# Layer 1 of a two-layer metaformer: silu(z) ahead of the scans, gating of each group at its end, output projection of five groups during the last passes

## The chip, the cores and the metric

The kernel runs on one core of one Trainium2 chip. The metric is the device time of one execution in microseconds (us). A stated time is the median of several executions. In the profile PE is TensorE (matmul), PEld its weight load, DVE is VectorE, ACT is ScalarE, POOL is GpSimd, and SP issues most of the DMAs. PEclk is the clock granted to TensorE as a share of full speed. A name such as L1216 is a line of the kernel whose profile is read; the two kernels have different line numbers.

## The reference

Two layers, each a two-dimensional state space block with a gate, then an MLP in simulated fp8. The change touches only the gate and the output projection of layer 1:

```python
# x: 1 x 64 x 64 x 96, D_INNER = 192, 16 states, L = 64*64 = 4096
def _L1_conv_ref(x, W_in, conv_w, conv_b, x_proj_w, dt_proj_w, dt_proj_b, A_logs, Ds, W_out):
    xz = x @ W_in.T
    xp, z = (xz[..., :D_INNER], xz[..., D_INNER:])
    xc = jax.nn.silu(conv3x3(xp) + conv_b)            # full 192 x 192 convolution
    # four directions: rows, columns, and both reversed
    # dts, Bs, Cs: projections of xc; delta = softplus(dts + dt_proj_b)
    # h = exp(delta*A)*h + (delta*u)*B ; y = sum over states of h*C, + Ds*u
    yy = y[0] + wh_y + inv_y[0] + invwh_y             # [..] directions summed
    yy = yy * jax.nn.silu(z)
    return yy @ W_out.T
# [..] then x = x + that, and t = t + ffn(layernorm(t))
```

## The kernel before

Layer 1 has four parts: convolution and projections, a stretch in which the first operands of the scans are loaded, 24 scan passes (six groups of 32 channels times four quarters of the states), and the tail. Constants: `P=128, L=4096, CH=512, NCH=8, SC=1024, NS=4, NG=6, NK=4, NQ=4, GC=32, CD=96, DI=192`. In a pass, 16 scans of 128x1024 run on VectorE; ScalarE makes the decays, GpSimd multiplies by B and C, and TensorE adds the four directions and folds the states into an accumulator `accs[g]`.

```python
def layer1(self, w):
    # [..] pools: up (u, xd, dtc), ps (2 PSUM), pc (4 PSUM), kp (sg), sp (z, dt, du, zz, p; 2 buffers each)
    for c in range(0, NCH, 4):
        self.conv_chunks(kp, ps, pc, u, c)
        self.project_chunks(sp, ps, u, c)      # u, dt, du, B, C to DRAM
    for g in range(2):
        nc.sync.dma_start(self.dt_d[1][g * P : g * P + GP[g], :], self.dtc[g])

def scans(self):
    # [..] st: dt0, dt1, du, x0..x2, xw, c, hs, h0, h1 of [P, L], three hc of [P, SC]
    def store(i):                              # y of a group to DRAM at the group's end
        g, k = passes[i]
        if k < NK - 1:
            return
        t = hcs[(NS * i + NS) % 3].rearrange("p (b t) -> p b t", t=CH)
        keep(nc.scalar.copy(t, accs[g]))
        to = self.y_d[GC * g : GC * g + GC, :].rearrange("c (b q t) -> q c b t", q=NQ, t=CH)
        for q in range(NQ):
            nc.sync.dma_start(to[q], t[GC * q : GC * q + GC])
    # [..] plan: which helper is issued after which scan of a pass

def tail(self, w, out):
    # [..] u, y and the layer's input xt are loaded back from DRAM
    def gate(c):
        s = chunk(c)
        for g in range(2):
            n = GP[g]
            nc.vector.scalar_tensor_tensor(
                y[g][:, s], u[g][:, s], self.tail_d4[g][0:n], y[g][:, s], ALU.mult, ALU.add)
            z = self.pa.tile([P, CH], F32, tag="a", name=f"z1{c}{g}")
            self.keep(nc.tensor.matmul(z[0:n], w_in[:, g * P : g * P + n], xt[:, s], start=True, stop=True))
            sg = self.tp.tile([P, CH], F32, tag="sg", name=f"sga{c}{g}")
            nc.scalar.activation(sg[0:n], z[0:n], AF.Sigmoid)
            nc.vector.tensor_tensor(sg[0:n], sg[0:n], z[0:n], ALU.mult)
            nc.gpsimd.tensor_tensor(y[g][:, s], y[g][:, s], sg[0:n], ALU.mult)
    def mixed(c):                              # output projection of one chunk of 512 tokens
        o = self.po.tile([P, 4, CD], F32, tag="o", name=f"o1{c}")
        for j in range(4):
            at = slice(c * CH + j, (c + 1) * CH, 4)        # every fourth token is a weight column
            for g in range(2):
                self.keep(nc.tensor.matmul(o[:, j, :], y[g][:, at], w_out[g], start=g == 0, stop=g == 1))
        nc.vector.tensor_tensor(self.res[:, c], self.res[:, c], o, ALU.add)
        self.mlp_norm(1, c)
    for c in range(NCH):
        gate(c)
    # [..] for each chunk in turn: mixed, mlp_turn (transpose), mlp_up, mlp_down, store
```

`keep` holds an instruction to the program order on its engine; what is not kept, the scheduler may move.

## Time and profile before

The kernel before takes 1683.67 us (1680.88 to 1685.94, three runs). The profiled execution has a span of 1672.6 us. I cut it where one thing becomes the next.

| stretch (us, profiled execution) | from | length |
|---|---|---|
| first store of dt of the last chunks to the issue of the load of x0s | 517.99 | 28.5 |
| issue of x0s to the first scan | 546.46 | 32.6 |
| the 24 passes of scans | 579.11 | 931.0 |
| end of the last scan to the last sum of states | 1510.13 | 19.2 |
| last sum of states to the end | 1529.36 | 143.2 |

The other lines of this profile on which the argument rests stand in the prediction below. A row of a timeline is: start, length, engine and line, operation, output and inputs, shapes, number of instructions; in brackets the idle time of the engine just ahead and what ended it. One more line of this kernel is from the view of a single source line and gives the shortest, median and longest duration in ns of the weight loads with which TensorE adds the directions inside the scans:

```profile
L1190 PEld LDWEIGHTS hs<-hss,ident x384: 186/190/338, 601.0 to 1522.1; 128*128 128x128 f32 x192
```

A load of 128 neighbouring columns takes 0.19 us here, wherever TensorE has its full clock (301 of the 384 loads), and 0.29 to 0.34 us where the granted clock is 0.50 (70 of them).

### The profile page before, as it was taken

Reading aid. Unit: us, or ns where it says so; the run is one execution under the profiler, and the core shown is the slowest. Engines: PE = TensorE matmul, PEld = TensorE weight load, DVE = VectorE, ACT = ScalarE, POOL = GpSimd, SP = SyncE. Lnnn points to the kernel's source line nnn. Section 1 sums busy time; section 2 is a strip of 40 time slices with the busy share of each in tenths; the row PEclk is TensorE's granted clock in tenths of the full one; section 3 lists DMA queues with packets and bytes.
Section 4 is the critical chain, followed back from the end, with each engine's and each line's share of the span. In section 5 each row is a group of like instructions: output and inputs, shape, how many; then the busy total and the mean of one; then the engine's idle time right before and its main releaser. Section 6 shows DMA issues by size and latency. Waiting matters only on the chain.

```text
span 1672.6 us, 11637 instructions
## 1 busy us (share of the span) xinstructions
PE 1199.6 (72%) x3518; PEld 487.2 (29%) x3518; DVE 1203.2 (72%) x921; ACT 874.5 (52%) x988; POOL 780.4 (47%) x435
## 2 busy tenths in 40 slices
PE   5969788799992047776667777677777666776986
PEld 2512344443430012222222222222222222222353
DVE  6595355400505199999999999999999999991634
ACT  5233243301405366667676777766676667752233
POOL 1001222100202447777777666777777687642522
PEclk9968766599995568888888787888888788888555
DMA  2121200001204802454355345433633563213400
GB/s 68 50 71 49 50 10 10 19 13 32 88 26 148 348 26 101 173 201 127 127 195 170 126 151 187 127 107 144 218 122 108 180 224 117 59 55 82 119 10 29
DMA packets 52011, 178.37 MB, mean 107 GB/s; under 512 B 18288, under 2 KB 23140, under 8 KB 44772
## 3 DMA queue, kind: packets, MB, share of 16 engines
q1 hardware_dynamic: 50356, 177.35, 32.3%
q8 instruction: 29, 0.48, 0.1%
q10 hardware_dynamic: 1584, 0.20, 0.1%
q14 instruction: 42, 0.34, 0.1%
HBM read 154.92 MB, written 22.56 MB: 106 GB/s over the span
## 4 chain that ended last, share of the span: by engine, by line
DVE 43%; PE 26%; ACT 6%; DMA 5%; issue 4%; POOL 3%; SPq 2%; DVEq 1%; POOLq 0%; ACTq 0%
DVE h0s L1173 13%; DVE h1s L1173 12%; DVE xws L1173 6%; PE cv L974 4%; DVE x0s L1173 4%; DVE x2s L1173 3%; DVE x1s L1173 3%; PE o L1336 3%; ACT da L1161 2%; PE cv L979 2%; PE z L1323 2%; PE cw L987 2%; DMA cs<-bc 2%; PE in L285 1%; PE o L455 1%
## 5 line engine op out<-in xcount | busy, mean ns | idle before, releaser
L1190 PE MATMUL hs<-hss,ident 128*128 128x512 f32 x384 | 233.5, 694 | 132.7 <-POOL hss L1179 87.2
L1161 ACT ACTIVATE da<-dt0s,a 128x1024 f32<-128x1024 f32 x168 | 187.7, 1117 | 137.5 <-DVE xws L1173 52.3
L1161 ACT ACTIVATE da<-dt1s,a 128x1024 f32<-128x1024 f32 x168 | 187.9, 1119 | 102.7 <-DVE xws L1173 69.6
L1179 POOL TENSOR_TENSOR hss<-h1s,xws 128x1024 f32<-128x1024 f32 x96 | 224.4, 2374 | 26.7 <-PE hs L1190 14.2
L1173 DVE TENSOR_TENSOR_SCAN xws<-da,xws 128x1024 f32<-128x1024 f32 x96 | 224.2, 2335 | 8.3
L1191 PE MATMUL hs<-h0s,ident 128*128 128x512 f32 x384 | 216.5, 648 | 5.1 <-DVE h0s L1173 5.1
L1173 DVE TENSOR_TENSOR_SCAN h1s<-da,h1s,xws 128x1024 f32<-128x1024 f32 x72 | 169.2, 2350 | 9.7 <-ACT da L1161 0.5
L1190 PEld LDWEIGHTS hs<-hss,ident 128*128 128x128 f32 x384 | 75.5, 215 | 274.4 <-issue 101.6
L1191 PEld LDWEIGHTS hs<-h0s,ident 128*128 128x128 f32 x384 | 81.0, 211 | 114.7 <-issue 103.4
L1203 POOL TENSOR_TENSOR hc0s<-hc0s,cs 128x1024 f32<-128x1024 f32 x32 | 75.3, 2355 | 79.9 <-ACT hc0s L1198 65.6
L1203 POOL TENSOR_TENSOR hc1s<-hc1s,cs 128x1024 f32<-128x1024 f32 x32 | 75.4, 2355 | 77.2 <-ACT hc1s L1198 65.8
L1203 POOL TENSOR_TENSOR hc2s<-hc2s,cs 128x1024 f32<-128x1024 f32 x32 | 75.3, 2354 | 76.3 <-ACT hc2s L1198 67.0
L1049 POOL TENSOR_TENSOR du<-u,dt 128x1024 f32<-128x1024 f32 x6 | 17.4, 2896 | 198.9 <-ACT z L691 109.8
L1214 PE MATMUL acc<-hc0s,fold 128*32 128x512 f32 x128 | 40.6, 719 | 75.2 <-POOL hc0s L1203 75.2
L1214 PE MATMUL acc<-hc1s,fold 128*32 128x512 f32 x128 | 40.6, 719 | 73.9 <-POOL hc1s L1203 73.9
L1144 POOL TENSOR_TENSOR x0s<-x0s,dus 128x1024 f32<-128x1024 f32 x32 | 75.0, 2355 | 34.4 <-DMA dus<-du 24.0
L1173 DVE TENSOR_TENSOR_SCAN h1s<-da,xws 128x1024 f32<-128x1024 f32 x24 | 54.5, 2271 | 48.6 <-DMA cs<-bc 45.6
L1214 PE MATMUL acc<-hc2s,fold 128*32 128x512 f32 x128 | 39.7, 704 | 68.6 <-POOL hc2s L1203 68.6
L1144 POOL TENSOR_TENSOR x2s<-x2s,dus 128x1024 f32<-128x1024 f32 x32 | 75.1, 2359 | 14.9 <-DMA cs<-bc 9.1
L1144 POOL TENSOR_TENSOR x1s<-x1s,dus 128x1024 f32<-128x1024 f32 x32 | 75.0, 2356 | 12.3 <-DMA cs<-bc 8.2
L1150 ACT COPY xws<-x0s 128x1024 f32<-128x1024 f32 x32 | 61.5, 1951 | 31.8 <-POOL x0s L1144 31.8
L1173 DVE TENSOR_TENSOR_SCAN x1s<-da,x1s 128x1024 f32<-128x1024 f32 x32 | 74.7, 2335 | 2.8
(245 smaller groups left out, 2433.7 us busy)
## 6 DMA issues: line engine op xcount, KB each, us to landing
cs<-bc SPq DMA_DIRECT2D x384, 128.0 KB
x0s<-bc SPq DMA_DIRECT2D x32, 512.0 KB
x1s<-bc SPq DMA_DIRECT2D x32, 512.0 KB
x2s<-bc SPq DMA_DIRECT2D x32, 512.0 KB
dus<-du SPq DMA_DIRECT2D x24, 512.0 KB
dt1s<-dt SPq DMA_DIRECT2D x40, 256.0 KB
dt0s<-dt SPq DMA_DIRECT2D x40, 256.0 KB
bce<-re SPq DMA_DIRECT2D x2, 1232.0 KB
```

The lines of the kernel that those rows point to most:

```text
L974: nc.tensor.matmul(t, cw[0][:, tap, 0:P], image(0, slice(0, P), n, tap), start=tap == 0, stop=False)
L979: nc.tensor.matmul(t, cw[1][r, tap, 0:P], image(1, r, n, tap), start=False, stop=tap == 8)
L1144: keep(nc.gpsimd.tensor_tensor(x, x, du[:, part[j]], ALU.mult))
L1150: keep(nc.scalar.copy(grid(xw)[:, w, :], cols(xs[i % 3])[:, w, :]))
L1161: nc.scalar.activation(das[i, s], dt[o][:, part[j]], AF.Exp, scale=self.a6[:, g, k : k + 1])
L1173: keep(nc.vector.tensor_tensor_scan(to, da, x, start, ALU.mult, ALU.add))
L1179: nc.gpsimd.tensor_tensor(cols(hs)[:, w, :], grid(first[1])[:, w, :], grid(xw)[:, w, :], ALU.add)
L1190: keep(nc.tensor.matmul(t, self.ident, hs[:, s], start=True, stop=False))
L1191: keep(nc.tensor.matmul(t, self.ident, first[0][:, s], start=False, stop=False))
L1203: keep(nc.gpsimd.tensor_tensor(t, t, c[:, part[j]], ALU.mult))
L1214: nc.tensor.matmul(accs[g][GC * q : GC * q + GC, m // NQ, :], self.fold4, hcs[(NS * i + a) % 3][:, h * CH : (h + 1) * CH], start=k == 0, s ...
L1336: nc.tensor.matmul(o[:, j, :], y[g][:, at], w_out[g], start=g == 0, stop=g == 1)
```

## The change

Two idle places were to be used. Between the projections and the first scan TensorE has nothing to do, so z, its sigmoid and their product move there and go to DRAM (`gate1`). During the scans TensorE and GpSimd have slack, so each group is gated at its own end, and the output projection of groups 0 to 4 runs in the last three passes. The tail keeps the projection of the last group's 32 channels and the MLP. To make room, C gets two tiles of a quarter of the length instead of one full tile.

```diff
@@ layer1
+            xt = zp.tile([CD, L], F32, tag="xt", name="xt1z")
+            nc.scalar.dma_start(xt, self.xn_d)
             for c in range(0, NCH, 4):
                 self.conv_chunks(kp, ps, pc, u, c)
                 self.project_chunks(sp, ps, u, c)
             # [..] stores of dtc
+            self.gate1(kp, sp, ps, xt)
+        # [..] in project_chunks, keep(...) around ScalarE's column copies of dt
+
+    def gate1(self, kp, sp, ps, xt):
+        # [..] silu: sigmoid on ScalarE (kept in order), product with z on VectorE
+        for i in range(6):
+            g = i // 4
+            sz = sp.tile([P, n], F32, tag="z", name=f"sz{i}")
+            for m in range(2):
+                t = ps.tile([P, CH], F32, tag="ps", name=f"z1{i}{m}")
+                # [..] one matmul, or two of 64 rows
+                silu(sz[:, m * CH : (m + 1) * CH], t, f"{i}{m}")
+            # [..] nc.scalar.dma_start(self.sz_d[..], sz[..])
@@ scans
-            xw, c, hs = (st.tile([P, L], ...) for t in ("xw", "c", "hs"))
+            xw, hs = (st.tile([P, L], ...) for t in ("xw", "hs"))
+            cs = [st.tile([P, SC], F32, tag=f"c{m}", name=f"c{m}s") for m in range(2)]
+            def load_gate(i, late): ...          # u and silu(z) of the group into gu, gz
+            def skip(i): ...                     # ScalarE: gu = gu * 4D
+            def fetch_y(i):
+                    keep(nc.scalar.copy(t, accs[g]))
+                    keep(nc.gpsimd.tensor_tensor(gu, gu, t, ALU.add))
             def store(i):
-                keep(nc.scalar.copy(t, accs[g]))
+                    keep(nc.gpsimd.tensor_tensor(gu, gu, gz, ALU.mult))
+                    # [..] gu to y_d
+            def early_out(m):
+                t = ph.tile([P, CH], F32, tag="hs", name=f"eo{m}")
+                for j in range(4):
+                    keep(nc.tensor.matmul(o[:, j], gu[:, b, j:CH:4], w0, start=True, stop=False))
+                    keep(nc.tensor.matmul(o[:, j], gz[0:GC, b, j:CH:4], w1, start=False, stop=True))
+            def early_fetch(m): ...              # ScalarE: PSUM to et
+            def early_add(m): ...                # GpSimd: res += et
+            def gate_last(i, a): ...             # VectorE: last group, a quarter at a time
+            at(gate_last, 18, 20, 23, 29)
-            at(load_c, 2, 5, 7, 13)
+            at(load_c, 7, 13, 17, 20)
+                    for f, at_slots in ((early_out, (8, 10, 11)), (early_add, (12, 13, 14)), (early_fetch, (9, 11, 13))):
+                        # [..] in passes 21, 22 and 23: three, three and two chunks
@@ tail
-            # [..] reloads of u, xt and y; gate(c) for all chunks
             def mixed(c):
                 for j in range(4):
-                    for g in range(2):
-                        nc.tensor.matmul(o[:, j, :], y[g][:, at], w_out[g], ...)
+                    nc.tensor.matmul(o[:, j, :], y[r, b, j:CH:4], w2[r], start=True, stop=True)
```

## The prediction

> **What bounds the kernel now.** I read the table of busy time by stretch first, with the cuts set where the chain of waits changes engine: convolution and projections of layer 1, the bubble before the first scan, the 24 scan passes, the last sums, the gate, and output projection with MLP.
>
> ```profile
> core 0: us, PE busy (x) PEld busy (x) DVE busy (x) ACT busy (x) POOL busy (x), PEclk, DMA share, GB/s
> 514.00:579.00 65.00, 0.00 (x0) 0.00 (x0) 19.17 (x14) 22.16 (x17) 27.28 (x11) 0.50 0.75 281
> 579.00:1510.00 931.00, 642.96 (x1489) 240.30 (x1490) 892.00 (x384) 639.57 (x619) 643.77 (x277) 0.83 0.41 139
> 1510.00:1530.00 20.00, 16.87 (x48) 6.06 (x46) 0.13 (x1) 4.02 (x7) 8.32 (x4) 1.00 0.00 0
> 1530.00:1574.00 44.00, 31.43 (x33) 6.49 (x33) 23.65 (x31) 10.66 (x17) 19.40 (x15) 0.51 0.77 191
> 1574.00:1673.00 99.00, 69.99 (x280) 48.60 (x280) 39.98 (x82) 32.19 (x66) 23.67 (x35) 0.50 0.04 16
> ```
>
> The scans (579 to 1510) are DVE alone: 384 scans in 931 us, 2.42 us from one to the next, 38.8 us for a pass of 16. The waits of DVE in that stretch confirm it:
>
> ```profile
> DVE h1s L1173 <- DMA cs<-bc: 45.6, 1, 45.6
> DVE h1s L1173 <- ACT da L1161: 3.5, 7, 0.6
> ```
>
> Only 3.5 us are lost inside; the 45.6 us are the wait for the first scan. PE, ACT and POOL are 69% busy there, so each has some 11 us free in a pass. What is left to win lies at the two ends. The timeline of PE shows the back end:
>
> ```profile
> 1528.31 1.05 PE L1214 MATMUL acc<-hc2s,fold 128*32 128x512 f32 x4 [2.50 <-POOL hc2s L1203]
> 1542.52 31.40 PE L1323 MATMUL z<-xta,tw_in 96*128 96x512 f32 x32 [13.16 <-DMA xta<-xn]
> 1573.85 11.43 PE L1336 MATMUL o<-two,ys 128*128 128x96 f32 x32
> 1591.32 0.66 PE L171 MATMUL tf<-identb,xb 128*96 128x128 bf16 x4 [6.04 <-POOL xb L1403]
> ...
> 1646.78 5.70 PE L1336 MATMUL o<-two,ys 128*128 128x96 f32 x16
> 1654.96 0.66 PE L171 MATMUL tf<-identb,xb 128*96 128x128 bf16 x4 [2.48 <-POOL xb L1403]
> ```
>
> From the last sum of states (1529.4) to the end (1672.6) are 143.2 us: 13.2 of reloading, 31.4 of z products, then the output projection, 16 instructions and 5.5 us for each of 8 chunks, in turn with the MLP. The front end, from the timelines of SP, POOL, ACT and DVE:
>
> ```profile
> 538.71 1.13 SPq L949 DMA_DIRECT2D dt<-dtc  x1
> 546.46 2.39 SPq L1117 DMA_DIRECT2D x0s<-bc  x4
> ...
> 559.87 9.23 POOL L1144 TENSOR_TENSOR x0s<-x0s,dus 128x1024 f32<-128x1024 f32 x4 [23.97 <-DMA dus<-du]
> ...
> 569.13 7.46 ACT L1150 COPY xws<-x0s 128x1024 f32<-128x1024 f32 x4 [31.77 <-POOL x0s L1144]
> ...
> 579.11 2.29 DVE L1173 TENSOR_TENSOR_SCAN h1s<-da,xws 128x1024 f32<-128x1024 f32 x1 [45.64 <-DMA cs<-bc]
> ```
>
> This is a serial chain: the load of x0s waits until the store of dtc frees its memory, and 32.6 us later (579.11 - 546.46) the first scan starts. PE does nothing here, ACT and DVE nothing from 538. So the bubble looks free for the gate, but only if x0s doesn't wait for it.
>
> **What the Trainium skill says.** "TensorE: Matmul & The Clock Gate", Part 1, has the array at half rate by default and after an idle window of some 3.4 us, and at full rate after as long a busy one. The trace agrees on the first half: 1.00 up to 1530, then 13.2 us idle, then 0.51. On the second it doesn't: 31 us of z products never raised it. I therefore price both new z products and the tail at the half clock. The same page, Part 2, step by step, says that a weight load's time follows the columns, not the rows; the trace agrees (the 6x128 and the 128x128 loads both took 0.18 to 0.19 us at full clock), so 32 rows in place of 128 and 64 make the projection cheaper by fewer instructions, not by cheaper ones. "ScalarE: Activation LUTs", What ACT_TABLE_LOAD costs, gives 1283 ns for a table; the trace has 1.28 us. The front has sigmoid's table already, so one load leaves the tail and none is added. "DMA: Bandwidth & Descriptors", Anatomy of one DMA, puts most of a fixed 2 us into the receipt of the write; I use it for the sz stores, as no row gives landing times.
>
> **The change part by part.**
>
> Tail, removed or moved. The reload and z products vanish: 1573.85 - 1529.4 = 44.4 us. The projection keeps only the last group's 32 channels: 8 instructions a chunk, not 16, so 8 x 0.344 (5.5 / 16) = 2.75 us. First two chunks: before, 17.5 us from 1573.85 to the first turn at 1591.32; after, 5.5 of products, and most of the norm, some 9 in all (the gate of the last quarter, two DVE operations of 0.7, runs beside the products). Turns one to seven: before 1654.96 - 1591.32 = 63.6 us, less six projections of 2.75, 47.1. But here the norm hid beneath a projection; in the built program the normalisation of every second chunk still stands behind the next chunk's residual add on DVE, so the 2.48 us wait before the turn stays and its neighbour gets one too: I add 4, 51. The end, 1654.96 to 1672.6, stays 17.6. Sum 9 + 51 + 17.6 = 78, against 143: **-65**.
>
> Front, added. The order of the built program and its semaphores settle this. PE's z products may run early, but ACT's sigmoids are kept behind the last dtc copy (ends 537.4). Twelve tiles, two PSUM buffers: at half clock a tile costs PE 1.7 us (two instructions of 0.85; before the tail made one in 1.95), sigmoid 0.6 and multiply 0.7 beside it, plus an ACT DMA issue a pair: about 3.5 us a pair, six pairs, 21, to 558.5. Two sz buffers mean that a pair also waits for the store two earlier, 512 KB among the 5 MB that already saturate the DMA until 546; that gives much the same pace. Last stores issue at 559 and land 2.5 to 3 later, 562. In the built program the load of x0s waits for exactly these last sz stores and stands behind seven of the loads for group 0's gate. So x0s goes at 562 in place of 546.46, the 32.6 us follow as before: **+15.5**.
>
> Scans. Two gate operations for each of five groups, 2.35 us each, stand on POOL at the end of a pass, where its plan has free slots; the early projection adds 16 instructions, some 3.5 us, to PE three times in a pass, in the last three passes; ACT gets a 0.5 us fetch for each, and near the end of a pass it has little room (seven of its waits already showed). I give two pass ends 1.5 us: **+3**. The multiplier C, loaded into two buffers and not four, has a whole POOL slot or more to land; nothing for it.
>
> Sum: -65 + 15.5 + 3 = -46.5; 1683.7 - 46.5 = 1637. I say 1636.
>
> **Rivals.** First, the gate really lies in the bubble: if its stores land by 550, the front costs 4 and the time is 1625. For it: PE idle 65 us. Against: the kept order on ACT and the semaphores. Second, the scans lose their pace: SP issues in order and now carries waits on POOL and PE among its loads, ACT stalls on the early products; at 2 us a pass for the last ten passes that is 20 us and 1654. Against: DVE has lost only 3.5 us so far with the other engines 31% idle. Third, MLP and norms become the bound of the tail: DVE and ACT need under 5 us a chunk, but in a chain of ten steps; at 10 us a turn, the tail gains 55, and 1646. Fourth, PE stays at full clock in the tail as it comes without an idle gap: 10 us better, 1626.
>
> **Range and chances.** The tail's gain is surely 44 and probably 60 to 75; the front costs 4 to 22; the scans 0 to 20. Together 1612 to 1662. Two per cent is 1650; it is missed only if two costs come out high: faster 0.79, same 0.19, slower 0.02.
>
> **What would show it.** First scan near 595 (before 579.1); the wait of SP for the sz stores; scans again 931 to 937 us with DVE waits under 8 us; from the last sum of states to the end 74 to 84 us, with 8 instructions of 0.34 us in each projection and the clock near 0.5. A first scan by 584, a tail still over 95 us or under 65, or DVE waits over 15 us inside the scans make a step wrong.

## The result, and the profile after

The changed kernel takes 1634.54 us (1632.23 to 1636.59, four runs), the kernel before in the same rounds 1682.28 us (four runs). The ratio is 0.9715, with a 95% interval from 0.9689 to 0.9741. A ratio is the mean time of one kernel's fast runs over that of the other's of the same rounds, so it is not quite the ratio of the medians.

The stretches of the profiled executions, 1672.6 and 1634.8 us long:

| stretch | before | after | difference |
|---|---|---|---|
| start to first store of dt | 518.0 | 520.0 | +2.0 |
| first store of dt to issue of x0s | 28.5 | 49.5 | +21.0 |
| issue of x0s to first scan | 32.6 | 33.3 | +0.7 |
| scans | 931.0 | 940.6 | +9.6 |
| last scan to last sum | 19.2 | 22.1 | +2.8 |
| last sum to end | 143.2 | 69.3 | -73.9 |
| sum | 1672.6 | 1634.8 | -37.8 |

The medians differ by 47.7 us and these two executions by 37.8: the profiled execution of the kernel before (1674.52 us) was faster than its four timed runs, that of the changed kernel (1636.59) was the slowest of its four. The +2.0 of the first row is noise, though the load of xt and the order kept on ScalarE's copies lie in it. The first conv matmul of layer 1 comes 5.3 us later, and the way from there to the store is 3.3 us shorter (181.1 against 184.4), as a stretch at a granted clock of 0.50 in the convolution lasts 3.4 us and not 10.2. `place` below has the convolution of the changed kernel and the 10.2 and 184.4 us of the kernel before. The first experiment shows how large such noise can be. I therefore argue with stretches, not with medians.

The table of busy time by stretch of the changed kernel, cut at its own borders (columns: stretch, length, then busy time and instructions of each engine, clock, share of DMA time, GB/s):

```profile
core 0: us, PE busy (x) PEld busy (x) DVE busy (x) ACT busy (x) POOL busy (x), PEclk, DMA share, GB/s
516.00:602.80 86.80, 21.96 (x32) 5.83 (x32) 27.22 (x26) 29.20 (x29) 27.29 (x11) 0.50 0.73 271
602.80:1543.50 940.70, 682.85 (x1614) 273.53 (x1615) 892.26 (x384) 647.57 (x631) 674.21 (x294) 0.82 0.44 144
1543.50:1565.50 22.00, 19.41 (x53) 7.04 (x51) 6.65 (x6) 3.86 (x7) 9.39 (x4) 1.00 0.16 48
1565.50:1634.80 69.30, 40.43 (x218) 29.12 (x216) 39.97 (x82) 31.66 (x65) 22.23 (x32) 0.51 0.07 24
```

The z products now stand in the first of these stretches, 22 us at half clock. VectorE still does 384 scans in 892 us of busy time, as before, but the stretch around them is 9.6 us longer. The waits of VectorE inside it (total us, times, longest):

```profile
DVE h1s L1216 <- ACT da L1204: 7.9, 16, 1.6
DVE x1s L1216 <- ACT da L1204: 1.9, 2, 1.0
DVE x0s L1216 <- ACT da L1204: 1.9, 2, 1.0
DVE h0s L1216 <- ACT da L1204: 1.8, 2, 1.0
```

With 1.0 us more for x2s they make 14.5 us, against 3.5 before. Some 11 of them fall after 1430, that is, in the last three passes. There the waits of ScalarE name its cause (the first line), and the view of the two lines of the early projection gives their weight loads:

```profile
ACT et L1328 <- PE eo L1318: 16.3, 8, 4.2
...
L1317 PEld LDWEIGHTS eo<-two,gus x64: 307/319/332, 1438.2 to 1533.4; 128*128 128x128 f32 x64
```

ScalarE waits 2 us for each of the eight early products and, working in order, is late with the decays. A load takes 0.32 us and not 0.19. The half clock doesn't explain it: 20 of the 64 loads fall at a granted clock of 1.00 and 38 at 0.50, and the median of both is 0.32. TensorE is busy 105.0 of the 105 us from 1425 to 1530, at a mean clock of 0.83. The first 21 passes take 815.4 us against 815.0 before, the last three 125.3 against 116.0: nearly all of the +9.6 is there.

The front end, from the timelines of SP, ACT and VectorE:

```profile
541.26 0.35 ACTq L984 DMA_DIRECT2D sz<-sz  x1
551.73 1.29 DVE L964 TENSOR_TENSOR sz<-z,sgz 128x512 f32<-128x512 f32 x2 [5.84 <-DMA sz<-sz]
564.78 1.37 ACTq L984 DMA_DIRECT2D sz<-sz  x2
569.50 2.40 SPq L1160 DMA_DIRECT2D x0s<-bc  x4
602.84 2.29 DVE L1216 TENSOR_TENSOR_SCAN h1s<-da,xws 128x1024 f32<-128x1024 f32 x1 [38.09 <-DMA x2s<-bc]
```

The first store of silu(z) is issued at 541.3; the product that needs its buffer again waits for it until 551.7. The later stores whose landing a wait shows took 2.6 to 3.6 us. The last stores are issued by 566.2, and x0s follows at 569.5.

The back end, from the timeline of TensorE:

```profile
1561.79 1.05 PE L1256 MATMUL acc<-hc1s,fold 128*32 128x512 f32 x4 [0.95 <-DVE gus L1343]
1564.49 1.05 PE L1256 MATMUL acc<-hc2s,fold 128*32 128x512 f32 x4 [1.64 <-DVE gus L1343]
1565.47 3.19 PE L1436 MATMUL o<-two,gus 32*128 32x96 f32 x16
1573.28 0.66 PE L171 MATMUL tf<-identb,xb 128*96 128x128 bf16 x4 [4.62 <-POOL xb L1497]
1611.49 2.18 PE L1436 MATMUL o<-two,gus 32*128 32x96 f32 x8
1616.94 0.66 PE L171 MATMUL tf<-identb,xb 128*96 128x128 bf16 x4 [3.27 <-POOL xb L1497]
```

The last sums wait for VectorE's gating, which is new. The projection of a chunk is 2.18 us where it was 5.5, and every second turn still waits 3.27 us for the norm.

### The profile page after: what moved, and what is told of

Same layout as the page of the kernel before. It is cut to its first block, busy times and chain, and to the rows that moved or that the text cites. A ratio compares the mean times of both kernels' runs of the same rounds, so it can differ in the third digit from the quotient of the medians.

```text
span 1634.8 us, 11885 instructions
## 1 busy us (share of the span) xinstructions
PE 1202.9 (74%) x3582; PEld 500.6 (31%) x3582; DVE 1194.5 (73%) x909; ACT 877.6 (54%) x995; POOL 789.5 (48%) x436
## 4 chain that ended last, share of the span: by engine, by line
DVE 40%; PE 31%; ACT 6%; issue 5%; DMA 4%; POOL 3%; DVEq 1%; SPq 0%; ACTq 0%; POOLq 0%
DVE h0s L1216 12%; DVE h1s L1216 10%; DVE xws L1216 7%; PE cv L1009 4%; DVE x0s L1216 3%; PE hs L1233 3%; DVE x1s L1216 3%; DVE x2s L1216 3%; PE hs L1234 2%; PE hs L1235 2%; PE cv L1014 2%; PE cw L1022 2%; ACT da L1204 2%; PE o L454 1%; PE o L455 1%
## 5 line engine op out<-in xcount | busy, mean ns | idle before, releaser
L1222 POOL TENSOR_TENSOR hss<-h1s,xws 128x1024 f32<-128x1024 f32 x96 | 224.4, 2372 | 28.2 <-PE hs L1233 15.5
L1187 POOL TENSOR_TENSOR x2s<-x2s,dus 128x1024 f32<-128x1024 f32 x32 | 75.1, 2361 | 20.8 <-DMA c1s<-bc 13.9
L1256 PE MATMUL acc<-hc2s,fold 128*32 128x512 f32 x128 | 39.8, 704 | 58.7 <-POOL hc2s L1245 57.0
L1216 DVE TENSOR_TENSOR_SCAN x0s<-da,x0s 128x1024 f32<-128x1024 f32 x32 | 74.7, 2335 | 4.5 <-ACT da L1204 1.9
L1216 DVE TENSOR_TENSOR_SCAN x2s<-da,x2s 128x1024 f32<-128x1024 f32 x32 | 74.7, 2335 | 3.7 <-ACT da L1204 1.0
L1193 ACT COPY xws<-x0s 128x1024 f32<-128x1024 f32 x32 | 61.6, 1955 | 28.8 <-DMA x1s<-bc 28.8
L1235 PE MATMUL hs<-x0s,ident 128*128 128x512 f32 x128 | 69.3, 624 | 0.2 <-DVE x0s L1216 0.2
```

The costliest lines, as they stand in the source:

```text
L1187: keep(nc.gpsimd.tensor_tensor(x, x, du[:, part[j]], ALU.mult))
L1193: keep(nc.scalar.copy(grid(xw)[:, w, :], cols(xs[i % 3])[:, w, :]))
L1216: keep(nc.vector.tensor_tensor_scan(to, da, x, start, ALU.mult, ALU.add))
L1222: nc.gpsimd.tensor_tensor(cols(hs)[:, w, :], grid(first[1])[:, w, :], grid(xw)[:, w, :], ALU.add)
L1235: keep(nc.tensor.matmul(t, self.ident, xs[i % 3][:, s], start=False, stop=True))
L1256: nc.tensor.matmul(accs[g][GC * q : GC * q + GC, m // NQ, :], self.fold4, hcs[(NS * i + a) % 3][:, h * CH : (h + 1) * CH], start=k == 0, s ...
```

## The experiments

Twelve kernels ran, on three chips. "First scan" below is always counted from the first store of dt of the last chunks, so that layer 0 doesn't disturb it: 61.1 us before, 82.8 after. Ratios are to the kernel before in the same rounds. ctrl shares its chip with place, front, z_only and, in later rounds, best_two; conv_gate, six_sz, x0_first and contig ran on a second chip, acc_split, best and best_place on a third. Across chips only stretches and ratios are compared.

**ctrl: the changed kernel again.** No edit.

> The changed kernel itself, unaltered, as the control of this chip: the stages should repeat (first scan 82.8 us after the first store of dt of the last chunks, scans 940.6 us, last scan to end 91.4 us), each within 1 us; the ratio to the kernel before about 0.9715.

1630.52 us, ratio 0.9754 (0.9731 to 0.9777). First scan 81.6, scans 941.9, last scan to end 91.3: the last as expected, the first two off by 1.3 us, so smaller differences of a stretch are not read below. Its profiled span, though, is 9.1 us shorter than the first one of the same program. The table of busy time shows where, in the first 80 us, first of ctrl and then of the earlier execution:

```profile
0.00:80.00 80.00, 60.36 (x416) 30.15 (x416) 50.29 (x108) 31.51 (x56) 7.33 (x40) 1.00 0.25 60
```

```profile
0.00:80.00 80.00, 61.76 (x342) 31.10 (x346) 42.27 (x99) 30.87 (x56) 6.79 (x40) 0.85 0.17 38
```

The same program was granted a clock of 1.00 once and 0.85 once, and in the same 80 us did 416 and 342 matmul instructions. The first conv matmul of layer 1 came at 329.9 and 338.9. Such differences can be in every median below, as noise of several us.

**conv_gate: the silu(z) block inside the convolution.**

```diff
             for c in range(0, NCH, 4):
                 self.conv_chunks(kp, ps, pc, u, c)
                 self.project_chunks(sp, ps, u, c)
+                if c == 0:
+                    self.gate1(kp, sp, ps, xt)
-            self.gate1(kp, sp, ps, xt)
```

> The changed kernel, with the silu(z) block called after the first four chunks of the convolution instead of after the last four, so that its matmuls, sigmoids, products and stores lie inside the stretch where TensorE convolves. Theory A (the 21.7 us that the first scan came later are the block itself, standing alone between the last projection and the first scan, at half the TensorE clock and with x0s waiting for its last stores): the first scan comes 11 to 18 us earlier than in the changed kernel (about 588 instead of 602.8; the matmuls still cost TensorE some 8 us inside the convolution) and the time falls to about 1620 (1616 to 1624). Rival B (the delay comes from the extra loads of u and z for group 0 that stand on the queue ahead of x0s, wherever the block is): the first scan comes no more than 5 us earlier, the time stays above 1628.

1635.38 us, ratio 0.9784 (0.9736 to 0.9832): nothing won. The front itself did what theory A said: x0s at 28.4 us and the first scan at 61.6, just as in the kernel before. But the convolution and projections, from the first conv matmul to that store of dt, took 206.7 us instead of 181.1. The groups of TensorE in that stretch:

```profile
L969 PE MATMUL z<-xt1z,w_in 96*128 96x512 f32 (+1 forms) x32 | 16.5, 769 | 6.6 <-DVE sz L965 6.6
L1015 PE MATMUL cv<-pad,cw 64*128 64x512 f32 x144 | 35.2, 629 | 0.0
```

16.5 us are the products, 6.6 a wait for a PSUM buffer (an accumulator that matmuls write to), and 3.2 lie in one group of conv matmuls (35.2 us, against 32.0 in ctrl), together 26.3, about what the stretch grew by. I had put some 8 us for it. Here, where TensorE is busy, the block costs its whole length; in the bubble it costs 21. So of the two places tried, the bubble was the better.

**six_sz: three pairs of buffers for the silu(z) tiles.**

```diff
-            sz = sp.tile([P, n], F32, tag="z", name=f"sz{i}")
+            sz = sp.tile([P, n], F32, tag=("z", "dt", "du")[i % 3], name=f"sz{i}")
```

> The changed kernel, with the six silu(z) tiles turned over three pairs of buffers (those of z, dt and du) instead of one pair, so that no product waits for an earlier store to land. Theory A1 (the block is paced by the landing of its stores, VectorE waited 5.84 us for one at 551.7): the wait of VectorE for the stores is gone, the last store is issued 4 to 8 us earlier (near 560 instead of 566) and the time falls by 4 to 8 us, to about 1629. Rival A2 (the block is paced by its own chain of matmul at half clock, sigmoid and product): the wait goes, but the last store comes less than 2 us earlier and the time stays within 2 us of 1634.5.

1631.64 us, ratio 0.9737 (0.9697 to 0.9776). First scan at 77.6 us: 5.2 earlier than in the first profile and 3.9 earlier than in ctrl. Theory A1 is supported by the stretch; the medians can't show so little.

**x0_first: loads in program order.** `keep(...)` around the loads of the scans and of the gate, so x0s, du and dt1 stand ahead of the loads of u and silu(z).

> The changed kernel, with the loads of the scans and of the gate held in program order on the queue, so that x0s, du and dt of the first pass stand ahead of the loads of u and silu(z) for group 0. Rival B (these loads hold x0s back): x0s is issued at about 562 and the first scan comes 5 to 8 us earlier, time about 1628. Theory A (x0s waits for the memory of the last silu(z) stores whatever stands ahead of it): x0s is issued within 2 us of 568; what is gained is only the transfer of those loads, 1 MB, about 3 to 4 us at the 271 GB/s of that stretch, time about 1631 (1629 to 1633).

1636.60 us, ratio 0.9769 (0.9721 to 0.9818). x0s at 48.3 and the first scan at 81.2, against 48.8 and 81.6 in ctrl. Rival B falls: the loads ahead of x0s don't hold it back. The 3 to 4 us for the transfer of those loads, which theory A gave, didn't come either.

**place: x0s, du and dt1 over memory that is free early.**

```diff
+            sa = inner.enter_context(tc.tile_pool(name="sa", bufs=1))
             st = inner.enter_context(tc.tile_pool(name="st", bufs=1))
-            dt = [st.tile(...) for o in range(2)]; du = st.tile(...); xs = [st.tile(...) for m in range(3)]
+            dt = [(st, sa)[o].tile(...) ...]; du = sa.tile(...); xs = [(sa, st, st)[m].tile(...) ...]   # hcs too
```

> The changed kernel with program order kept on the loads, and with x0s, du, dt1 and the three small product tiles in a pool of their own, over the memory of u, xd and the column copies of dt, which is free before the silu(z) block. Theory A (x0s waits for memory that the silu(z) block holds): x0s is issued by 550, 19 us earlier, and the first scan comes 8 to 20 us earlier, less than the full 21 because three megabytes of silu(z) stores share the queues. Rival F (the loads and the stores share a fixed number of transfers in flight, so the second to eighth loads wait for stores of silu(z) anyway): the first x0s load is early, but the fourth and the loads of du wait for stores until 562 to 567, and the first scan comes less than 5 us earlier, time within 5 us of the control.

1632.31 us, ratio 0.9752 (0.9726 to 0.9778). The first x0s goes at 31.9 us instead of 48.8, but the first scan only at 75.1, 6.5 us earlier: less than theory A gave (8 to 20) and more than F (under 5). The time doesn't show even that: ctrl has the ratio 0.9754 in the same rounds, and either is known to about 0.25%. The waits of the SP queue from 550 to 580 say why:

```profile
SPq L1161 <- DMA sz<-sz: 15.0, 5, 5.7
```

In the built program the transfers take turns with eight semaphores (counters on which an instruction waits), whichever queue issues them, and a transfer waits for the one that had its semaphore before. So the loads of x0s and du wait five times for stores of silu(z) that need not come first. Both theories hold in part: memory was the wait that ended last in the changed kernel, and transfers in flight are the one behind it.

**front: the block with fewer waits of its own.** Program order of the loads, six buffers (tags z, zz, p), and the z products on the convolution's four PSUM buffers.

```diff
-                t = ps.tile([P, CH], F32, tag="ps", name=f"z1{i}{m}")
+                t = pc.tile([P, CH], F32, tag="cv", name=f"z1{i}{m}")
```

> The changed kernel with program order kept on the loads, the six silu(z) tiles over three pairs of buffers, and the z matmuls writing to the four accumulators of the convolution, which are idle by then, instead of the two of the projections: nothing else of the block is changed. Theory G (the block's 30 us are mostly waits of TensorE for the two accumulators, 25.6 us of idle time in the trace, and not its own 22 us of matmuls): the last silu(z) store is issued near 553 instead of 566 and the first scan comes 10 to 14 us earlier than in the control; time 9 to 14 us less. Rival A2 (the half clock of the matmuls and their 22 us set the pace): the first scan comes no more than 6 us earlier, as with the six tiles alone (5.2 us there).

1625.57 us, ratio 0.9711 (0.9689 to 0.9733), on ctrl's chip in the same rounds as ctrl's 0.9754. x0s at 42.0 and the first scan at 74.8: 6.8 us earlier than in ctrl, where the six buffers alone gave 3.9. Theory G (10 to 14) is too large by half, and A2 (6 at most) a little too small. TensorE is no longer what paces it: 16 matmul instructions run ahead in 7.5 us. The stores run from 22.2 to 39.3 us after the dt store; the first can't come sooner, as ScalarE has the softplus and the column copies until then. Some 13.7 us over the kernel before are left: one pass of sigmoid, product and store behind those copies, in which one sigmoid of ScalarE still stands 3.9 us behind an earlier store. That is read from the timeline; no run took it away.

**contig: the early weights from neighbouring columns.** Its output is wrong, which doesn't matter for the time.

```diff
-                    keep(nc.tensor.matmul(o[:, j], gu[:, b, j:CH:4], w0, start=True, stop=False))
-                    keep(nc.tensor.matmul(o[:, j], gz[0:GC, b, j:CH:4], w1, start=False, stop=True))
+                    keep(nc.tensor.matmul(o[:, j], gu[:, b, j * P : j * P + P], w0, start=True, stop=False))
+                    keep(nc.tensor.matmul(o[:, j], gz[0:GC, b, j * P : j * P + P], w1, start=False, stop=True))
```

> The changed kernel, with the weights of the early out_proj matmuls taken as 128 neighbouring columns instead of every fourth column (the result is wrong on purpose; same number, shapes and order of instructions). Theory C (the weight load of columns with a stride of four, 0.30 to 0.33 us, makes the early out_proj 5.7 us a chunk on a TensorE that is full in the last three passes, and ScalarE, waiting in order for it, holds up the decays of the scans): a load takes about 0.20 us, a chunk about 3.7 us, the waits of the scans for the decays fall by 5 to 8 us and the time by as much, to about 1628. Rival D (the load time follows the shape and the clock, not the stride): loads stay at 0.30 to 0.33 us and the time within 1 us. Rival E (the scans lose their time to GpSimd's gate work and the copies of ScalarE, not to TensorE): loads are shorter but the time falls by less than 2 us.

1624.04 us, ratio 0.9701 (0.9657 to 0.9745). The scans take 932.0 us, 8.6 less than in the first profile and 9.9 less than in ctrl. The weight loads, and the only wait of the scans for the decays that is left:

```profile
L1317 PEld LDWEIGHTS eo<-two,gus x64: 186/189/333, 1431.4 to 1514.9; 128*128 128x128 f32 x64
...
DVE h1s L1216 <- ACT da L1204: 4.0, 7, 0.7
```

0.189 us is the load time of the identity in the kernel before, and 4.0 us is near its wait of 3.5. 39 of the 64 loads fall at a clock of 1.00 and take 0.19; the 22 at 0.50 take 0.29 to 0.33, no less than with the step. ScalarE waits 0.5 us for the early products, not 16.3. Theory C stands, with more than it gave (waits down by 10.5 us); D and E fall, as the shape, the number and the order of all instructions are the same. One thing does differ: the mean clock of the last three passes was 0.81 in the changed kernel and is 0.85 here. It isn't the cause: acc_split below keeps the step and was granted 0.83, z_only has no early projection and was granted 0.84, and the three passes took 122.9 and 116.0 us.

**z_only: no early projection.** The groups are gated as in the change, but y is loaded in the tail and all six groups are projected there, 24 instructions a chunk (correct).

> The silu(z) block and the gating of the groups as in the changed kernel, but no early out_proj: the tail loads the gated y of groups 0 to 4 and does the projection of all six groups, 24 matmul instructions a chunk instead of 8 (correct result). Theory H (the early out_proj is worth the 16 instructions that leave each turn of a tail bound by TensorE, 0.27 us each, and costs the scans 8.6 us): the scans take 932 us instead of 940.6, last scan to end takes 120 to 128 us instead of 91.4, time about 1661 on the first chip, 1.2 to 1.9 per cent above the control. Rival I (the tail is bound by VectorE and the norm chain, so the matmuls were mostly hidden): last scan to end grows by less than 15 us and the time is within 8 us of the control.

1658.33 us, ratio 0.9917 (0.9898 to 0.9936), 1.7% above ctrl. The scans take 931.1 us, so gating on GpSimd, the extra copies on ScalarE and the two small C tiles cost them nothing. Last scan to end is 127.2 us against 91.3. Theory H stands on all three numbers: the early projection wins 35.9 us behind the scans and costs 10.8 in them. From the end of the last scan to the last sum are 21.7 us, only 0.4 less than in ctrl, and the last sum has the same wait for the gating:

```profile
1548.62 1.05 PE L1256 MATMUL acc<-hc2s,fold 128*32 128x512 f32 x4 [1.65 <-DVE gus L1343]
```

**acc_split: two accumulator tiles, and the third quarter gated late.**

```diff
-                    accs[g] = pq.tile([P, NCH // NQ, CH], F32, tag="acc", name=f"acc{g}")
+                    accs[g] = [pq.tile([P, CH], F32, tag=f"acc{b}", name=f"acc{g}{b}") for b in range(nb)]
-            at(gate_last, 18, 20, 23, 29)
+            at(gate_last, 18, 20, 29, 29)
```

> The changed kernel, with the accumulator of a group as two tiles of one bank each instead of one tile of two, and the gating of the third quarter of the last group put after the last sum of states, so that the last two sums of states wait for no gating on VectorE. Theory J (the 2.8 us between last scan and last sum of states are TensorE's waits of 0.95 and 1.64 us for VectorE's gating, a dependence through the shared accumulator tile): both waits vanish, last scan to last sum falls from 22.1 to about 19.5 us and the time by about 2.5 us. Rival K (the sums wait for GpSimd's products anyway, and the DVE wait only stands in for them): the waits turn to GpSimd and the stretch stays within 0.7 us.

1628.99 us, ratio 0.9704 (0.9669 to 0.9738). From the timeline of TensorE, the last sum:

```profile
1561.16 1.92 PE L1256 MATMUL acc<-hc2s,fold 128*32 128x512 f32 x4 [2.21 <-POOL hc2s L1245]
```

The waits for VectorE are gone, but the stretch is 21.4 us, 0.7 less than in ctrl. In number this is rival K's case, and theory J is mostly wrong; but the clock has a part in it. The split wins 1.4 us between ScalarE's copy of the first quarter's sums and the start of the last sum (19.8 us instead of 21.2), but 0.9 are lost in the last sum itself, which runs at half clock (1.92 instead of 1.05 us). And the late gating gives more back in the tail: last sum to end is 71.7 us instead of 69.2, as the quarter gated late stands on VectorE ahead of the first norm, and the first turn comes 10.2 us after the last sum instead of 7.75. The rest of the +2.8, 1.7 us, is work that TensorE still owes when the last scan ends: ScalarE's copy of the first sums starts 0.2 us before the end of the last scan in the changed kernel, 1.9 us before it in the kernel before. The early projection is not the main reason, as z_only, without it, starts that copy 0.6 us before. What goes with it is a stretch of 10.2 us at a granted clock of 0.50, which ends 6.7 us before the end of the last scan in the kernel before and 4.1 to 4.2 us before it in z_only and ctrl. No run moved that alone, so the cause of the 1.7 us stays open.

**best, best_place, best_two: the findings together.** All three have front and a right version of contig: the product that gates a group writes y in the order (j, token), so that the weight columns lie side by side, and a tile `gy` takes the memory of `et`.

```diff
-                    keep(nc.gpsimd.tensor_tensor(gu, gu, gz, ALU.mult))
+                    keep(nc.gpsimd.tensor_tensor(gy.rearrange("p b (j t) -> p b t j", j=4),
+                                                 gu.rearrange("p b (t j) -> p b t j", j=4),
+                                                 gz.rearrange("p b (t j) -> p b t j", j=4), ALU.mult))
# [..] the same in gate_last; early_out and mixed take columns j*P : j*P + P
```

best adds acc_split; best_place adds the pool of place as well; best_two has the pool and leaves acc_split out.

> Front (loads in program order, six silu(z) buffers, z matmuls on the idle accumulators of the convolution), the split accumulator, and a gated y that is written in the order j, token by its last product, so that the weights of the early and of the last out_proj are neighbouring columns and the result is right. If the causes add up: front 6.7 us, weights 8.6 us in the scans, split 2.5 us, together 18 us under the control, some 1612.5 on the chip of the control, ratio to the kernel before about 0.9645. If the permuted writes of the products (stride of 512 bytes) cost GpSimd much, the scans take more than 935 us instead of 932.

> The same, with x0s, du, dt1 and the small product tiles in a pool of their own over memory that is free before the silu(z) block. If the loads wait only for transfers in flight, the earlier stores of this block let the loads go 4 to 7 us earlier than in the kernel without the extra pool, time 4 to 7 us less. If the front is by now bound by ScalarE's block and by the bytes to be moved, within 2 us of it.

> The version with the front, the pool of its own and the permuted gated y, but with the gating of the last group as in the changed kernel, one accumulator tile and each quarter gated right after its sum. If the third quarter's gating after the last sum cost the tail what the split had saved (last sum to first turn 10.2 us there against 7.75 in the control), last scan to last sum returns to about 21.5 us and last sum to end falls from 71.8 to about 69: the time is some 1 us lower than the version with the split, ratio to the kernel before about 0.962. If the split itself was a gain, the time is 2 to 3 us higher.

| kernel | time | ratio to before | first scan | scans | last scan to last sum | last sum to end |
|---|---|---|---|---|---|---|
| ctrl | 1630.52 | 0.9754 (0.9731 to 0.9777) | 81.6 | 941.9 | 22.1 | 69.2 |
| best | 1616.94 | 0.9640 (0.9613 to 0.9666) | 74.6 | 934.2 | 18.4 | 71.8 |
| best_place | 1616.01 | 0.9623 (0.9594 to 0.9651) | 71.7 | 934.9 | 19.5 | 71.9 |
| best_two | 1618.07 | 0.9612 (0.9588 to 0.9635) | 72.3 | 934.1 | 22.0 | 68.3 |

All are correct, and all beat both kernels. By stretches the sums are 15.8, 16.8 and 18.1 us under ctrl. For best 18 were given, so its causes added up to a little less; best_place fell short of its 22 to 25. The extra pool won 2.9 us at the front (4 to 7 were given), the permuted products cost GpSimd almost nothing (2.39 us against 2.36), and acc_split won and lost the same few us. Which of the three is fastest the intervals don't tell.

## Why the prediction was right or wrong

The time, 1636.0 against 1634.5, was right, and so were the mechanisms of front and tail; that of the scans was not, and the last sums were missing. The sizes were off: three terms were too good by 6.2, 6.6 and 2.8 us, and one too bad by 8.9. By stretches the change is worth 39.8 us (37.8 and the 2.0 of noise), not the 46.5 of the sum. That the time agrees so closely is luck twice: the errors cancel in part, and noise, as of layer 0 in ctrl, hides the rest. On ctrl's chip the medians differ by 42.8 us, not 47.7. Of its own signs it missed the first scan (near 595, measured 602.8), the scans (931 to 937 us), their waits (under 8 us, measured 14.5), the end (74 to 84 us) and the 0.34 us per instruction; none of the signs that were to make a step wrong came.

- **Front, +15.5 predicted, +21.7 measured.** The step that failed is the pace: "about 3.5 us a pair, six pairs, 21", with the landing of the stores said to give "much the same pace". From the first issue of a store to the last were 24.9 us for five pairs, some 5 each. The last two of them kept the 3.5; the second took 7.1, as the first store landed only after 10 us (541.3 to 551.7) and there were two buffers, and six_sz took 3.9 to 5.2 us off by more buffers alone. The 2.5 to 3 us that the prediction gave for a landing were near for later stores (2.6 to 3.6), not for the first. That x0s waits for the stores was right, and place and x0_first show it; the 32.6 us after it came as 33.3. The first rival, that the gate is nearly free in the bubble, was wrong, and the one other place tried for the whole block (conv_gate) was not cheaper.
- **Scans, +3 predicted, +9.6 measured.** The step that failed is the place: the 3 us were given to "two pass ends", and the early projection was taken to fit into the "some 11 us free in a pass". The pass ends cost nothing (the first 21 passes grew by less than 0.5 us); the last three passes grew by 9.3. The mis-sized term is "16 instructions, some 3.5 us, to PE". They keep TensorE busy for 5.1 to 5.75 us, so that three chunks in a pass are some 17 us and not 10.5. The weights are every fourth column, and at full clock such a load takes 0.32 us instead of 0.19. With neighbouring columns the 16 instructions take 3.2 us at full clock, up to 5.4 at half, 4.0 in the mean, and the scans 932.0: the estimate was near for weights of that kind. I had read the load time from the identity's and from the tail's rows, which are at half clock, where the two kinds can't be told apart: 0.324 us with the step in the changed tail, 0.328 without it in best. The Trainium skill, "SBUF — State Buffer", in the note on cachelines under Door 1: The DMA port swizzle, says that lines have 16 bytes and that each access in a new line pays. A step of four fp32 is just that. The runs show the cost of the step; that the lines are its cause, no run shows. GpSimd, which I also suspected, cost nothing (z_only 931.1).
- **Last scan to last sum, 0 predicted, +2.8 measured.** The prediction had no such step. It is made of two things: 1.1 us for the sums' waits on the gating, which acc_split took away, and 1.7 of TensorE's backlog, of which z_only still has 1.3 without an early projection. Its cause stays open.
- **Tail, -65 predicted, -73.9 measured.** Two terms were too large. An instruction of the last projection takes 0.272 us and not 0.344, and the six turns between 1573.28 and 1616.94 take 43.7 us where I had 51. The rule that one of two turns waits for the norm was right (3.27 us); the 4 us added for a second wait didn't come. The first turn came 7.75 us after the last sum (9 predicted), the end took 17.9 (17.6). z_only splits the gain: 37.7 us come from the tail without z, the gate and most of the reload (it still loads y, and projects with 24 instructions a chunk), and 36.3 more from the early projection.

Of the rivals, the second (the scans lose their pace) came true in part, for the last three passes and not for ten. The third and fourth did not: the tail gained 74 and stayed at a clock of 0.51.

What stays open: the 13.7 us of the front that no variant took away, the share of them that the semaphores' turns make, the 1.7 us of backlog at the last sums, and some 2 us of the scans in the best versions (934 against 932).

## What to carry to other kernels

Before work is moved onto an engine "with slack", price its instructions from rows with the same access pattern and the same clock: here one stride in the weights was the difference between a free projection and 10 us. Work that is late on an in-order engine is paid by whoever stands behind it there, so look for the copy that waits, not only for the engine that is full. And an idle stretch is only free up to the transfers and buffers that its successor waits for; count the stores in flight before moving a block ahead of a chain of loads.

## What the Trainium skill lacked or had wrong

- "TensorE: Matmul & The Clock Gate", LDWEIGHTS (loading the stationary operand), lets the time of a weight load follow the columns alone. For fp32 at full clock 128 columns took 0.189 us side by side and 0.319 us with a step of four; the page has no word on what the step costs. At half clock there was no such gap (0.31 to 0.33 us with the step, 0.29 to 0.33 without, in contig).
- The same page, Part 1, promises the full rate after some 3.4 us of sustained work. In the kernel before, 31.4 us of z products in a row stayed at 0.50; in the changed kernel the tail, where TensorE is busy 40 of 69 us, was at 0.51, and the 105 us from 1425 to 1530, where it is never idle, had 0.83 in the mean. The first 80 us of one program were granted 1.00 in one execution and 0.85 in another, which moved the time by 9 us.
- "DMA: Bandwidth & Descriptors", Anatomy of one DMA, has a fixed cost of some 2 us, fitted to DMAs issued from GpSimd; the prediction used it for stores issued from ScalarE. In a stretch with 271 GB/s, the first store of half a megabyte that ScalarE issued took 10 us from its issue to its landing, later ones 2.6 to 3.6; the page has no figure for a store that is issued behind others.
